# Two stacked cross-attention layers on one core: the key work of the second pair of batches moved by half a slot

## Chip, cores, metric

The kernel runs on one core of a Trainium2 chip. The metric is the device time of one execution in microseconds. It is taken as the median of several executions. All engines named below are those of the one core: PE (matrix products), ACT (scalar engine), DVE (vector engine), POOL (GpSimd), and SP, which here only issues DMA transfers. ACT issues a few small transfers too.

## What is computed

Two cross-attention layers follow each other. The input x has 16 batches of 256 positions and 320 channels; the context has 16 batches of 256 rows of 512, of which the first layer takes 77 rows as text and the remaining 179 as image tokens, and the second layer takes all but the last 4 rows as text. There are 20 heads of 16 channels. The first layer, cut to what matters:

```python
q = hidden_states @ Wq
k_text = text @ Wk
v_text = text @ Wv
probs = softmax(einsum('bhqd,bhkd->bhqk', q_h, k_h) * scale)
text_out = einsum('bhqk,bhkd->bhqd', probs, v_h)
ip_k = ip @ Wk_ip
ip_v = ip @ Wv_ip
scores = einsum('bhqd,bhkd->bhqk', q_h, ip_k_h) * scale
text_probs = softmax(einsum('bqc,bkc->bqk', q, k_text) * scale)
q_sem = einsum('bqk,bkc->bqc', text_probs, text)
sem = einsum('bqc,bnc->bqn', q_sem, ip) * scale
ip_probs = softmax(scores + SEM_SCALE * sem[:, None]) * spatial_mask
hs = text_out + einsum('bhqk,bhkd->bhqd', ip_probs, ip_v_h)
out = hs @ Wout + bout + residual
```

The second layer is built alike, with a semantic term per head that is normalised, and takes the first one's output.

## The kernel before

**Precision.** Every large product is made of three products of halves. A float32 operand is cast to a high half by ACT (line 147), and the rest is subtracted out as a low half by DVE or POOL (line 148). `prod` (line 205) then adds high by high, high by low and low by high: with four tiles of the contraction that is 12 matrix instructions into one PSUM bank.

**Slots.** A slot is one group of four heads of one batch; layer 0 has 80 slots (16 batches of 5 groups), layer 1 another 80. The main loop at the end of `xattn2` goes through the slots and issues for each of them a fixed sequence. In layer 0 (`slot0`) this is: the row maxima of slot k+1 turned on PE and sent into the query stack by four small DMAs issued by ACT (`maxima0`, L660, L662, L664); the scores of slot k+2, with two reductions by DVE (`score0`, L652, L653, L654); the turned scores of slot k (L676) with two exponentials on ACT (L679) and two multiplies on POOL (L682); then the fill point k+0.2; the weighted sum of slot k-1 (`attend0`, L709) with a transpose and small operations on DVE (`settle0`, L720 to L726) and a small add on POOL (L727); scores and turned scores for the second half of the rows; the loads of the stacks of slot k+4 on SP (`stacks0`); and the fill points k+0.6 and k+1.0.

**Tasks.** All other work is put into generators, called tasks. Each has a list of due times in slots, one for each of its steps (`task`, line 962). At a fill point (`fill`, line 990) every step that is due runs, earliest due time first. A step that needs another task's result runs that task as far as needed. Tasks that matter here are, for a pair of batches c: `k0` (keys and image keys of the pair, `keys0`), `q0` (queries of one batch, `queries0`), `m0t` and `v0` (token products and values), `s0` (semantic term), `c0` (closing of a batch).

**The steps of `k0` for the second pair (c = 1).** `context` loads four tiles of the context in its first step. Each of the next four steps splits one tile into halves, one cast on ACT and one subtraction on DVE (`halves`). Then come six steps, each with 12 products, a split of the result and either a copy on POOL (L318, after the text keys) or two stores of the keys to DRAM issued by SP (`keys_out`, after the image keys). The text keys' products have `wA` as their weights in the profile and 192 columns, the image keys' have `wB` and 360. The pair's keys are first read back by the stack loads issued in slot 6.

**Queries.** A batch's `q0` loads x into `xq`, splits it into `hq` (cast on ACT L517, low part on POOL L518, third tile on DVE L519), and projects it in three steps of 8 products (L528, `hq` by `wE`). The closing of a batch gathers the heads' output into `hT` (L739), splits it into `ho` (ACT L517, DVE L518, L519) and projects that (L528, `ho` by `wF`).

**Order.** The instructions of PE stand in the order in which the loop issues them. For the main loop the order of ACT, DVE, POOL and SP is set by a scheduler that estimates when each instruction will be ready; only within the start-up (`begin`) are these four pinned too. Each engine executes its own instructions in order. Two score banks (`T`), one bank for weighted sums (`P`), three for everything else (`X`) and one double bank for scores (`S`) are in PSUM; the loads of raw weights and context go through two buffers `rawc` and two buffers `raw`, each of which is free again when its subtraction is done; the keys go through two buffers `kst`.

The list of due times that the change touches, and the task that uses it:

```python
FIRST = {"k0": [-1, 0.2, 0.6, 0.6, 1, 1.2, 1.6, 1.6, 2, 2.2, 2.6], "s0": [...]}
task(("k0", c), FIRST["k0"] if c == 1 else shifted(n, ...), ...)
```

The pairs c = 2 to 7 take their times from `shifted`, and are not touched. Toward the end of layer 0, tasks `w6` and `w2` load the weights of the second layer (`wB` again for the image values, from `in_wvi`; `wE` for the queries, from `in_wq`) through the same `rawc` buffers.

Of the kernel before, what the change touches and what calls it, by code (L numbers as in the profile page):

```python
# [48 lines left out]
def xattn2(  # L49
# [249 lines left out]
    def keys0(c):  # L299
        if c not in ct0:  # L300
            tiles = context(2 * c, 2, 0.25)
            yield next(tiles)
            get("v0", 2 * c - 1)
            get("m0t", 2 * c - 1)
            ct0[c] = yield from tiles
        ct = ct0[c]
        kt = kts[c] = buf("kb", [128, 3, 2, 2, 96], FR, name="kt")
        for m in range(3):
            ms = slice(m * 128, (m + 1) * 128)
            kst = buf("kst", [128, 2, 2, S], FR, bufs=SIZES["KST"])  # L310
            for w, lo, hi, a, z in ((wk0, 0, 96, 0, T0), (wki0, T0 - 1, S, T0, S)):
                kp = bank()[:, : 2 * (hi - lo)].rearrange("p (b t) -> p b t", b=2)
                prod(kp, lambda s, k: w(s, k, ms), lambda s, k: ct(s, k)[:, :, lo:hi], 4)
                halves(kst[:, 0, :, a:z], kst[:, 1, :, a:z], kp[:, :, a - lo : z - lo])
                if a:
                    keys_out(kd[0][c], m, kst)
                else:
                    nc.gpsimd.tensor_copy(kt[:, m, :, :, :T0], f(kst[:, :, :, :T0]))  # L318
                yield
# [642 lines left out]
    def task(key, times, make, *needs):  # L962
        tasks[key] = [times, 0, make, needs, len(tasks)]
# [38 lines left out]
    def shifted(n, *times):  # L1002

        return [RAMP(n + t) for t in times]

    resid0 = []

    FIRST = {"k0": [-1, 0.2, 0.6, 0.6, 1, 1.2, 1.6, 1.6, 2, 2.2, 2.6], "s0": [-1, -1, -1, -1, -1, 0.2, 0.6]}
    for c in range(B // 2):
        n, k = 10 * c, [("k0", c)] if c else []  # L1010
        task(("k0", c), FIRST["k0"] if c == 1 else shifted(n, -14.4, -13.3, -13, -12.4, -12, -10.8, -10.4, -9.8, -9.4, -8.8, -8.4), (lambda c=c: keys0(c)) if c else keys_first,
             *([("w4", 0)] if c > 1 else []))
# [172 lines left out]
```

## Time and profile before

| | |
|---|---|
| median of 3 runs | 1636.12 us (1634.38, 1636.12, 1638.09) |
| the profiled execution's own time | 1630.48 us |
| its span, first to last instruction | 1628.7 us |
| PE busy | 1533.9 us (94%) |
| PE weight loads | 1232.8 us (76%) |
| DVE busy | 1209.1 us (74%) |
| POOL busy | 1189.4 us (73%) |
| ACT busy | 830.2 us (51%) |
| mean granted clock of PE | 0.974 |
| main chain that ended last | PE 52%, DVE 15%, POOL 11%, DMA 9%, ACT 6% |

Busy shares of PE overstate its work, since matrix instructions overlap. Over 40 equal slices PE is at nine tenths or more in most; the lower ones are the first (start-up), the 14th, 16th and 17th, and these lie between 529 and 692 us; layer 1's first slot begins at 744.0 us. The clock row of the page shows 9 nearly everywhere, 7 in the second slice (41 to 81 us) and 8 in the 17th and the last. Slot 0 begins at 55.1 us, slot 1 at 62.3, slot 2 at 84.7, slot 3 at 96.4 and slot 4 at 101.4.

How to read what follows: a timeline line gives the start in us, the length, the engine, the line of the kernel, the operation and its tiles, and how many of a kind follow each other; in brackets the idle time of the engine ahead of it and what ended it. "ACTq" and "SPq" are the issuing of transfers by these engines.

### The profile page before, as it was taken

The page shows a single profiled execution, that of the slowest core. Times are in us where ns is not written, and L with a number is a line of the kernel's source. Part 1 is how long each engine was busy: PE and PEld are TensorE (multiplying, and loading weights), DVE is VectorE, ACT ScalarE, POOL GpSimd, SP SyncE. Part 2 cuts the span into 40 slices and gives each one's busy share as a digit, 9 for nine tenths or more (in the row PEclk, how much of TensorE's full clock was granted, in tenths as well). Part 3 has the DMA queues.
Part 4 walks back from the last instruction along what each step waited for, and adds up shares of the span by engine and source line. Part 5 has one row for each costly group of instructions (what it writes and reads, how often), then busy time and mean ns, then how long its engine had stood idle before and what let it go on. Part 6 is the DMA issues. An engine that isn't in the chain of part 4 may idle for free.

```text
span 1628.7 us, 36230 instructions
## 1 busy us (share of the span) xinstructions
PE 1533.9 (94%) x13306; PEld 1232.8 (76%) x13306; DVE 1209.1 (74%) x2410; ACT 830.2 (51%) x1797; POOL 1189.4 (73%) x1147
## 2 busy tenths in 40 slices
PE   7899999999999898789999999999999999999996
PEld 6677878787878777577777777777777777777765
DVE  5567777777777668778877787778777877778685
ACT  5345455555555545445555555555554555555462
POOL 3358787878787767777678767866877687668676
PEclk9799999999999999899999999999999999999998
DMA  7767677767676666665514342433244334323301
GB/s 218 201 203 203 199 193 219 202 204 206 202 208 198 181 206 172 164 187 171 159 62 129 108 139 84 135 110 125 89 134 120 110 103 127 127 89 102 108 26 45
DMA packets 235741, 243.06 MB, mean 149 GB/s; under 512 B 19050, under 2 KB 219468, under 8 KB 235564
## 3 DMA queue, kind: packets, MB, share of 16 engines
q1 hardware_dynamic: 233356, 239.44, 49.4%
q8 instruction: 106, 1.74, 0.4%
q10 hardware_dynamic: 2208, 1.30, 0.3%
q14 instruction: 71, 0.58, 0.1%
HBM read 116.78 MB, written 88.18 MB: 126 GB/s over the span
## 4 chain that ended last, share of the span: by engine, by line
PE 52%; DVE 15%; POOL 11%; DMA 9%; ACT 6%; issue 4%; SPq 2%; ACTq 0%; POOLq 0%; DVEq 0%
PE X L205 15%; PE X L814 9%; PE X L528 7%; PE P L709 5%; POOL wt L805 4%; PE S L652 3%; POOL P L682 3%; PE P L823 3%; DMA qs<-qd 3%; PE P L826 2%; PE T L676 2%; PE T L775 2%; DVE wt L815 2%; DMA kd<-kst 2%; DVE mn L781 2%
## 5 line engine op out<-in xcount | busy, mean ns | idle before, releaser
L682 POOL TENSOR_TENSOR P<-P,rs 128x512 f32<-128x512 f32 x320 | 413.2, 1312 | 157.4 <-ACT P L679 157.0
L805 POOL TENSOR_TENSOR wt<-P,ctb 128x512 f32<-128x512 f32 x320 | 422.4, 1336 | 120.3 <-ACT ctb L804 118.7
L814 PE MATMUL X<-ctb,gm 128*128 128x512 f32 x1120 | 328.8, 411 | 2.5 <-DVE wt L815 2.5
L679 ACT ACTIVATE P<-T 128x512 f32<-128x512 f32 x320 | 175.9, 595 | 221.4 <-PE T L676 106.1
L786 ACT ACTIVATE P<-T 128x512 f32<-128x512 f32 x320 | 174.2, 597 | 144.1 <-PE T L775 123.3
L815 DVE TENSOR_TENSOR wt<-X,wt 128x512 f32<-128x512 f32 x320 | 216.7, 678 | 24.9 <-PE X L814 22.5
L804 ACT ACTIVATE ctb<-P 128x512 fp32r<-128x512 f32 x320 | 195.7, 631 | 73.1 <-PE X L814 57.9
L814 PEld LDWEIGHTS X<-ctb,gm 128*128 128x128 f32 x1120 | 188.8, 188 | 49.4 <-DVE wt L815 5.2
L781 DVE TENSOR_REDUCE mn<-S 128x4 fp32r<-128x1008 f32 x160 | 191.1, 1195 | 0.8 <-PE S L780 0.8
L654 DVE TENSOR_REDUCE mn<-S 128x4 fp32r<-128x716 f32 x160 | 142.6, 891 | 0.0
L676 PE MATMUL T<-qs,ks 127*128 127x256 f32 x640 | 112.1, 295 | 22.0 <-DMA qs<-mt 10.2
L709 PE MATMUL P<-P,vr 128*32 128x256 f32 x1920 | 129.4, 404 | 2.2 <-DVE mx L581 2.2
L652 PE MATMUL S<-ks,qs 125*128 125x256 f32 x640 | 117.4, 307 | 5.4 <-DVE mn L654 2.0
L652 PEld LDWEIGHTS S<-ks,qs 125*128 125x128 f32 x640 | 88.2, 194 | 41.8 <-issue 34.0
L894 POOL TENSOR_TENSOR r<-u,rs 128x40 f32<-128x40 f32 (+2 forms) x17 | 108.7, 6394 | 14.8 <-DVE u L891 14.7
L528 PE MATMUL X<-ho,wF 128*128 128x256 f32 x768 | 112.8, 290 | 6.4 <-DVE ho L518 3.0
L528 PE MATMUL X<-hq,wE 128*128 128x256 f32 x768 | 110.1, 287 | 7.5 <-ACT hq L517 3.2
L676 PEld LDWEIGHTS T<-qs,ks 127*128 127x128 f32 x640 | 92.8, 198 | 27.0 <-DVE tmp L726 11.6
L528 PEld LDWEIGHTS X<-ho,wF 128*128 128x128 f32 x768 | 103.5, 195 | 12.1 <-DVE ho L518 4.7
L528 PEld LDWEIGHTS X<-hq,wE 128*128 128x128 f32 x768 | 102.4, 193 | 12.0 <-ACT hq L517 3.6
L205 PE MATMUL X<-cta,wA 128*128 128x252 f32 (+1 forms) x720 | 100.6, 286 | 8.7 <-ACT wA L147 6.3
L205 PEld LDWEIGHTS X<-cta,wA 128*128 128x128 f32 x720 | 93.8, 194 | 15.2 <-ACT wA L147 6.5
(197 smaller groups left out, 2807.5 us busy)
## 6 DMA issues: line engine op xcount, KB each, us to landing
qd<-q SPq DMA_DIRECT2D x96, 384.0 KB
qs<-tph SPq DMA_DIRECT2D x64, 308.0 KB
kd<-kst SPq DMA_DIRECT2D x73, 256.0 KB
rawc<-in_cT_dram SPq DMA_DIRECT2D x60, 256.0 KB
qs<-qd SPq DMA_DIRECT2D x80, 192.0 KB
ks<-kd SPq DMA_DIRECT2D x80, 192.0 KB
ks<-kd SPq DMA_DIRECT2D x160, 96.0 KB
qs<-qd SPq DMA_DIRECT2D x160, 96.0 KB
```

Source lines behind the costliest of these rows:

```text
L205: last = mm(out, lhs(a, k), rhs(b, k), start=i == 0, stop=i == len(terms) - 1)
L528: mm(pp, w(s, k, slice(m * 128, (m + 1) * 128)), a[:, t], start=i == 0, stop=i == len(terms) - 1)
L652: mm(sp[:, h], Q[: XROW + T0, h, t * 128 : (t + 1) * 128], K[: XROW + T0, h], start=True, stop=True)
L676: mm(st[p][:, j], K[:KS0, 2 * p + j, t * 128 : (t + 1) * 128], Q[:KS0, 2 * p + j], start=True, stop=True)
L679: exp = anchor(nc.scalar.activation(pt, st[p], AF.Exp, scale=SCALE))
L682: anchor(nc.gpsimd.tensor_mul(pt, pt, rs[:, t : t + 1].to_broadcast([128, 2, S])))
L709: mm(pv[32 * s : 32 * s + 32, o : o + S], v[:, vt, h : h + 32], P[k, s // 2][:, t, s % 2], start=vt < 2, stop=vt != 1,)
L781: anchor(nc.vector.tensor_reduce(maxes[k + 2][:, t], sp[:, :, :T1], axis=AX.X, op=ALU.max))
L804: nc.scalar.activation(R[k, u][:, t], P[k, u][:, t], AF.Copy, scale=0.5)
L805: anchor(nc.gpsimd.tensor_sub(W[k, u][:, t], P[k, u][:, t], f(R[k, u][:, t])))
L814: mm(yp, gm[:, gb], R[k, u][:, kt], start=i == 0, stop=i == len(blocks[n]) - 1)
L815: nc.vector.tensor_mul(W[k, u][:, n], yp, W[k, u][:, n])
```

## The change

One list of eleven due times is replaced. Nothing else is edited; the number of instructions on PE is the same.

```diff
-    FIRST = {"k0": [-1, 0.2, 0.6, 0.6, 1, 1.2, 1.6, 1.6, 2, 2.2, 2.6], "s0": [-1, -1, -1, -1, -1, 0.2, 0.6]}
+    FIRST = {"k0": [-1, 0.6, 0.6, 1, 1.2, 1.6, 2, 2, 2.2, 2.6, 2.6], "s0": [-1, -1, -1, -1, -1, 0.2, 0.6]}
```

Step by step, for the second pair's keys (m is the third of the key channels):

| step | due before | due now |
|---|---|---|
| loads of four context tiles | -1 | -1 |
| halves of tiles 1, 2, 3, 4 | 0.2, 0.6, 0.6, 1 | 0.6, 0.6, 1, 1.2 |
| text keys, image keys, m = 0 | 1.2, 1.6 | 1.6, 2 |
| text keys, image keys, m = 1 | 1.6, 2 | 2, 2.2 |
| text keys, image keys, m = 2 | 2.2, 2.6 | 2.6, 2.6 |

On PE this puts the first 12 key products behind slot 1's weighted sum and its second scores and turned scores, and the later ones behind what stood after them, the first step of the queries of batch 2 among it. On the other four engines the scheduler decides anew; its order differs from the one before in slots 1 to 3, in some single places of later slots, and in a stretch around the change of layers (from about slot 68 to slot 85).

## The prediction

> **What bounds the kernel now.** I read the page's busy shares first (PE 94% of the span), then the clock over the first 240 us, then TensorE's own timeline where the moved work stands, then the queues that feed it. The edit touches the second to fourth slot, 63 to 101 us of the span. There PE is not limited by its work: it waits in short gaps, and for 20 us it runs at half clock. First the windows of 4 us; the third number from the end is the granted clock:
>
> ```profile
> 64.00:68.00 4.00, 3.47 (x12) 2.70 (x12) 1.97 (x4) 2.62 (x6) 0.55 (x1) 0.50 0.96 320
> 72.00:76.00 4.00, 4.00 (x29) 2.10 (x30) 0.86 (x2) 0.29 (x1) 0.44 (x1) 0.50 0.22 61
> 76.00:80.00 4.00, 4.00 (x26) 4.00 (x26) 2.71 (x7) 2.27 (x4) 2.31 (x2) 0.81 0.17 49
> ```
>
> The clock is 0.50 until about 77.2, though PE has no gap after 71.94: some 5.3 us of unbroken work before it comes back. The timeline of PE (start, length, instruction, and in brackets the idle time before it):
>
> ```profile
> 66.78 0.96 PE L205 MATMUL X<-cta,wA 128*128 128x192 f32 x3 [0.20 <-DVE cta L148]
> 68.57 0.74 PE L205 MATMUL X<-cta,wA 128*128 128x192 f32 x2 [0.84 <-DVE cta L148]
> 70.25 1.03 PE L205 MATMUL X<-ctb,wA 128*128 128x192 f32 x3 [0.73 <-DVE ctb L148]
> 71.94 0.74 PE L205 MATMUL X<-ctb,wA 128*128 128x192 f32 x2 [0.66 <-DVE ctb L148]
> 72.61 2.79 PE L709 MATMUL P<-P,vr 128*32 128x256 f32 x24
> ...
> 81.77 0.51 PE L528 MATMUL X<-hq,wE 128*128 128x256 f32 x2 [0.82 <-POOL hq L518]
> ```
>
> The first twelve key products wait four times for context halves (2.43 us together) and hold up L709, whose inputs POOL had finished at 64.54. The query projection L528 waits 0.82 for POOL. What stands before it on ACT and POOL:
>
> ```profile
> 70.09 3.63 ACTq L664 DMA_DIRECT2D qs<-mt  x3
> 73.82 0.29 ACT L147 CAST kst<-X 128x154 fp32r<-128x154 f32 x1 [3.12 <-DMA qs<-mt]
> 77.01 1.09 ACT L679 ACTIVATE P<-T 128x512 f32<-128x512 f32 x2 [2.90 <-PE T L676]
> 77.98 0.84 ACT L517 CAST hq<-xq 128x768 fp32r<-128x768 f32 x1
> ```
>
> ACT issues three small DMAs until 73.72, and only then serves the slot's exponentials, the hq cast and, through POOL, hq's low half.
>
> **First place: slots 0 to 3.** By the order of both programs, PE's instructions are the same in number; the key products move behind L709, S and T of slot 1, and eight of the query products now come before 24 of the key products.
> - Removed: the four gaps, 0.20 + 0.84 + 0.73 + 0.66 = 2.43 us. L709 starts at 66.0, ends at 68.7 (2.7 at half clock), S takes 1.15, T 0.85: 70.7.
> - The moved products then wait only for the last low half. DVE now does it behind the transpose (0.72) and two reduces (1.3) of that slot: from 70.2 to 72.1, then 0.7 to 1.15. The products end at 73.2.
> - Added: the query products come next. ACT is free at 73.72; two exponentials 1.09, hq cast 0.84: 75.6. POOL: two multiplies 2.80 from 74.4, the small add 0.45 that now stands between them, hq 1.27: 78.7. One product can go at 75.7, the rest at 78.7. The gap is 73.2 to 78.7, 5.5 less 0.2, where before it was 2.43 + 0.82 = 3.25: 2.1 us more. Behind the waiting instruction stand 24 key products and slot 2's L660, S and T; ACT's and POOL's next slot waits for these.
> - The clock: by the rows above it is back some 4.5 to 5.3 us after work resumes, near 83.5. Until then seven query products take 1.5 and twelve key products 3.4 (before, at 78.34, six took 1.14). Adding up: m1's twelve 1.32, L660/S/T 1.15, twelve 1.97, L709 1.43, S and T 1.15 give 90.6 for the T that ended at 89.87. That is +0.7, and twelve products (1.32) are still to do: +2.05 at the start of slot 3 (96.41 before).
> - What follows can swallow part. In slots 3 and 4 PE waits 1.50 for DVE and 2.20 before L709 at 106.77. Both hang on ACT's cast of wF at 100.02, which stands behind slot 3's exponentials; these follow PE by 2 us, and lose 0.7 of that in the DMA issue that was late anyway (98.91). I take **+1.4**. Low end -0.5: were the three DMA issues 0.57 each, as at 85.61, instead of 1.21, everything from ACT on would be 1.9 earlier. High end +2.6: nothing swallowed and the clock back 0.5 later.
> - DMAs moved: two key stores per third, 0.5 to 4 us later on SP, behind the load of xq now (0.86 to issue). Their reader, slot 6's stack, comes some 20 us after; cover is ample, and without it the price would be one such store's landing, 5 us. The kst casts and subtractions (0.29 to 0.53 each) fall on ACT and DVE while PE is the later one: nothing.
>
> The Trainium skill, "TensorE: Matmul & The Clock Gate" (section "Why this matters for your kernels"), asks for no PE-idle gaps above about 3 us, since one idle window sends the clock to half: that speaks against putting four short gaps into one. By its window of about 3.4 us the half-rate work would cost 1.7 us; this trace, where gaps of 0.7 to 1.9 us were enough to keep 0.50 for 20 us, makes it 2.2 to 2.6.
>
> **Second place: the change of layers.** The scheduler places all engines but PE, and its different start shifts two decisions near 650 to 690 us:
>
> ```profile
> 667.09 0.62 ACT L147 CAST wB<-rawc 128x512 fp32r<-128x512 f32 x1 [2.75 <-DMA rawc<-in_wvi_dram]
> ...
> 674.27 0.83 ACT L517 CAST ho<-hT 128x768 fp32r<-128x768 f32 x1 [1.08 <-DVE hT L739]
> ...
> 678.27 0.51 PE L528 MATMUL X<-ho,wF 128*128 128x256 f32 x2 [0.20 <-DVE ho L519]
> ...
> 684.41 0.23 PE L660 MATMUL X<-ident_r,mn 128*8 128x128 f32 x1 [2.04 <-DVE mn L654]
> ```
>
> - The third load of value weights now stands ahead of four stack loads on SP (issued 661.05 before, some 656.2 now, since DVE's subtraction that frees its buffer goes ahead of the transpose). Its 6 us then end at 661 to 662, ACT does not sit 2.75 us, and the T that ended at 667.04 ends near 663.5: -3.5.
> - Against it, the layer output ho is made later: POOL's copy L729 stands behind two more multiplies (2.5), the transpose L739 behind a subtraction of wE (1.56), ACT's cast behind another cast and two DMA issues. Working through: cast at 677.4, last part by DVE at 680.4, with PE ready at 674.5. PE idles 3.7 and then starts at half clock: the eight products end at 680.7 instead of 678.7, L709 2.72 and S 1.15 instead of 1.43 and 0.66, reduces 1.3: the L660 of 684.41 comes at 686.1. I take **+1.7**. Ends: -3.3 if ho is in time and the head start stays; +3.5 if ho is late and the early load gains nothing.
>
> **Third place: first stacks of layer 1.** On SP one of the three query stores now goes behind the load of xc (issue 1.18). The query rows, loaded at 759.06, wait for all three; ACT waited 4.18 for these, PE 0.51. I take **+1.0**, ends 0 and +2. The other swaps (single transposes, small adds) stand beside PE work of 1.4 to 3.5 us: nothing, or one instruction's 0.4 us each without that cover.
>
> **The sum.** 1.4 + 1.7 + 1.0 = +4.1 us. On the profiled execution's own 1630.48 (span 1628.7 and 1.8 around it) that is 1634.6; that execution is 5.6 below the median of the three runs, 1636.12, so the forecast is 1640.2. Later slots pass a delay on: they are a chain of PE and its feeders without slack that depends on the start.
>
> **The rivals.**
> - A, the forecast: 1640.2, own range 1637 to 1644. For it: PE stops at hq and at ho, each with its supplier's place in the queue. Chance 0.55, of which 0.10 falls within 0.2%.
> - B, not slower: the early weight load wins. Place: 656 to 676 us. Price: the head start of 3.5 us stays, with 1.4 paid at the start: 1634.0. It decides if ho's cast still comes by about 674.5. For it: the 2.75 us wait of ACT and 20 us without PE between 640 and 720 (by windows of 20 us), so there is something to win. Against it: the chain that makes ho is already 0.20 late today. Chance 0.22: 0.13 faster, 0.09 within.
> - C, the change does nothing that lasts: the waits of 1.50 and 2.20 swallow the start and the second place is level: 1636.1 to 1637.5. Against it: those waits hang on ACT, which follows PE. Chance 0.13.
> - D, all high ends: 2.6 + 3.5 + 2.0 = 8.1: 1644.2. For it: half clock was held for 20 us once. Chance 0.10.
>
> **How the numbers follow.** 0.2% is 3.3 us, about what a measurement of this kernel can tell. Slower: 0.45 + 0.10 = 0.55. Within: 0.10 + 0.09 + 0.13 = 0.32. Faster: 0.13. The sums of the ends are -0.5 - 3.3 + 0 = -3.8 (1632.3) and +8.1 (1644.2); with the spread of a median the range is 1632 to 1645.
>
> **What would show it.** Right: L709 of slot 0 near 66; one PE gap of 4 to 6 us before an L528 with the releaser POOL hq L518; clock 0.50 again in 79 to 83; slot 3's L660 some 2 us late; the third weight load issued before 658; a PE gap of 3 us or more before L528 on ho. Wrong: ACT's three DMA issues taking 1.7 us, or hq's low half before 76; ho's cast before 675; the layer-1 start earlier than before by more than 1 us.

## The result, and the profile after

| | changed | before |
|---|---|---|
| median | 1637.05 us (1632.61 to 1646.04, 12 runs) | 1633.47 us (1628.77 to 1638.09, 12 runs) |
| ratio | 1.0025, 95% interval 1.0013 to 1.0037 | |
| the profiled execution | 1646.04 us, span 1644.2 | 1630.48 us, span 1628.7 |

The change costs 3.6 us between the medians. A second measurement beside the experiments gave 1.0036 (1.0022 to 1.0049). The profiled execution of the changed kernel is the longest of its twelve, so its 15.5 us more than the profiled one of before are mostly not the change, and the traces must be compared stage by stage. For that I use the starts of L660 (L792 from row 80 on, in layer 1); each row has two such products, and the start of a row is here that of the second. A row is named by the slot whose maxima L660 makes; the instruction stands in the slot before, so the prediction's "slot 3's L660" is row 4. In the expectations below, slot numbers from 60 on are rows. Start of a row, less the same in the first trace of before (us):

| row | 0 | 2 | 4 | 6 | 42 | 66 | 72 | 74 | 76 | 78 | 84 | 157 |
|---|---|---|---|---|---|---|---|---|---|---|---|---|
| changed, first trace | 4.10 | 4.11 | 5.48 | 3.31 | 8.13 | 9.05 | 3.95 | 9.69 | 11.17 | 15.67 | 14.81 | 14.83 |
| changed, second trace | 2.50 | 2.50 | 3.36 | 1.14 | 2.22 | 3.12 | -1.59 | 5.37 | 6.90 | 9.40 | 8.55 | 8.62 |

Rows 0 to 2 lie before the change, and rows 6 to 66 have the same order of PE: what comes up there differs from one execution to the next. Both traces agree on two things: nothing is left of the start by row 6 (0.8 and 1.4 us less than at row 2), and 5.4 to 5.8 us come up between rows 66 and 84, at the change of layers.

PE at the start (timeline of the changed kernel: start, length, instruction, idle time ahead and what ended it):

```profile
68.52 2.18 PE L709 MATMUL P<-P,vr 128*32 128x256 f32 x24
...
75.16 0.47 PE L205 MATMUL X<-ctb,wA 128*128 128x192 f32 x2 [1.81 <-DVE ctb L148]
78.14 0.58 PE L528 MATMUL X<-hq,wE 128*128 128x256 f32 x1 [2.51 <-ACT hq L517]
81.40 1.86 PE L528 MATMUL X<-hq,wE 128*128 128x256 f32 x7 [2.69 <-POOL hq L518]
83.06 2.00 PE L205 MATMUL X<-cta,wB 128*128 128x360 f32 x6
```

L709 no longer waits behind the key products. These now wait 0.17 and 1.81, and the query product behind them waits for the ACT and then the POOL part of hq, 2.51 and 2.69. The windows of the same trace (third number from the end: granted clock) show what follows:

```profile
72.00:76.00 4.00, 1.65 (x11) 1.13 (x9) 3.87 (x8) 0.15 (x1) 1.84 (x2) 1.00 0.61 119
76.00:80.00 4.00, 0.58 (x1) 0.29 (x1) 0.71 (x2) 2.00 (x4) 3.05 (x3) 0.60 0.61 169
80.00:84.00 4.00, 2.60 (x11) 2.60 (x12) 0.29 (x1) 0.37 (x1) 1.74 (x3) 0.50 0.55 145
```

The clock reads 1.00 while PE has 1.65 us of work in 4, 0.60 while it has 0.58, and 0.50 when the work comes. ACT's timeline shows why hq is late, as forecast:

```profile
71.54 4.69 ACTq L664 DMA_DIRECT2D qs<-mt  x3
76.28 1.09 ACT L679 ACTIVATE P<-T 128x512 f32<-128x512 f32 x2 [4.12 <-DMA qs<-mt]
77.25 0.83 ACT L517 CAST hq<-xq 128x768 fp32r<-128x768 f32 x1
```

The change of layers, in the timeline of the changed kernel, engines together:

```profile
661.73 0.79 PE L676 MATMUL T<-qs,ks 127*128 127x256 f32 x2 [3.87 <-DVE tmp L726]
...
669.06 0.62 ACT L147 CAST wB<-rawc 128x512 fp32r<-128x512 f32 x1 [0.55 <-DMA rawc<-in_wvi_dram]
...
682.78 3.41 DVE L148 TENSOR_TENSOR wE<-rawc,wE 128x384 fp32r<-128x384 f32 x1
686.12 0.43 DVE L739 STREAM_TRANSPOSE hT<-hsn 128x256 f32<-128x256 f32 x1
686.58 0.83 ACT L517 CAST ho<-hT 128x768 fp32r<-128x768 f32 x1 [3.22 <-DVE hT L739]
687.47 2.59 PE L528 MATMUL X<-ho,wF 128*128 128x256 f32 x8 [5.45 <-ACT ho L517]
...
731.60 0.77 PE L676 MATMUL T<-qs,ks 127*128 127x256 f32 x2 [3.84 <-DVE P L724]
```

ACT's wait for the value weights falls from 2.75 to 0.55: the early load works, and row 72 is 5.1 us better than row 66 (4.7 in the second trace). Then PE waits 5.45 for ho, and the gain is gone by row 74. Both were forecast. The last line was not: 3.84 us before the last two of the four products of T (two banks of two), and 2.25 in the second trace, where the trace of before has the four in one piece. It has a wait of the same kind earlier, as the changed kernel has (the second trace of the changed kernel, then two lines of the trace of before):

```profile
725.57 0.48 PE L676 MATMUL T<-qs,ks 127*128 127x256 f32 x2 [2.25 <-DVE P L724]
```

```profile
652.04 0.80 PE L676 MATMUL T<-qs,ks 127*128 127x256 f32 x2 [3.98 <-DVE tmp L726]
...
717.59 0.63 PE L676 MATMUL T<-qs,ks 127*128 127x256 f32 x4
```

T reads qs and ks, which are there. What it waits for on DVE is a reader of P or S, which is no operand of T: the sign of a shared buffer. The built programs tell which PSUM bank each tile was given. The banks are not fixed per kind of tile (the numbers of banks given above for T, P, X and S say only how many of each may be in use at once); the scheduler hands out the eight of them by its own estimate of when each is free:

| tile | what its bank held last, before | what its bank held last, changed | PE's idle time ahead of it |
|---|---|---|---|
| T, row 70, first half, second bank | the last P | the last P | 3.98; changed 3.87 and 3.86 |
| X of L528 on ho, row 73 | a T | the last P | 0; changed 5.45 and 5.50, under the wait for ho |
| T, row 76, second half, first bank | the S just made | the S just made | 1.47; changed 1.47 and 1.47 |
| T, row 77, second half, second bank | a T | the S just made | 0; changed 3.84 and 2.25 |

S is read by L653 and L654. At row 77 these stand behind the split of the layer output (timeline of DVE, changed kernel):

```profile
727.22 1.54 DVE L518 TENSOR_TENSOR ho<-hT,ho 128x512 fp32r<-128x512 f32 x1
728.68 1.48 DVE L519 SCALAR_TENSOR_TENSOR ho<-ho,tmask,hT 128x256 fp32r<-128x256 f32 x1
730.08 0.25 DVE L723 RECIPROCAL P<-nt 128x16 f32<-128x16 f32 x1
730.24 0.41 DVE L653 TENSOR_REDUCE mn<-S 128x4 fp32r<-128x308 f32 x1
730.58 0.88 DVE L654 TENSOR_REDUCE mn<-S 128x4 fp32r<-128x716 f32 x1
```

L654 ends at 731.46, and T starts at 731.60; the releaser printed, L724, is merely the next on DVE. So there are two candidates for the cost at the change of layers: the order of the instructions, as forecast, or the banks.

### The profile page after: what moved, and what is told of

It reads as the page before. It is cut to its first block, busy times and chain, and to the rows that moved or that the text cites. A ratio compares the mean times of both kernels' runs of the same rounds, so it can differ in the third digit from the quotient of the medians.

```text
span 1644.2 us, 36224 instructions
## 1 busy us (share of the span) xinstructions
PE 1540.4 (94%) x13306; PEld 1240.0 (75%) x13306; DVE 1208.7 (74%) x2410; ACT 830.8 (51%) x1797; POOL 1188.2 (72%) x1147
## 4 chain that ended last, share of the span: by engine, by line
PE 54%; DVE 15%; POOL 10%; DMA 8%; ACT 5%; issue 4%; SPq 1%; ACTq 0%; POOLq 0%; DVEq 0%
PE X L205 17%; PE X L814 9%; PE X L528 7%; PE P L709 5%; POOL wt L805 4%; PE S L652 3%; PE P L823 3%; PE T L676 3%; POOL P L682 3%; PE P L826 3%; PE T L775 2%; DMA qs<-mt 2%; DVE wt L815 2%; DVE mn L781 2%; DVE ho L518 2%
## 5 line engine op out<-in xcount | busy, mean ns | idle before, releaser
L654 DVE TENSOR_REDUCE mn<-S 128x4 fp32r<-128x716 f32 x160 | 142.6, 891 | 0.0
L709 PE MATMUL P<-P,vr 128*32 128x256 f32 x1920 | 130.2, 407 | 1.5 <-DVE mx L581 1.5
L528 PE MATMUL X<-hq,wE 128*128 128x256 f32 x768 | 114.2, 294 | 13.1 <-ACT hq L517 6.1
L528 PE MATMUL X<-ho,wF 128*128 128x256 f32 x768 | 113.3, 291 | 11.7 <-ACT ho L517 6.9
L528 PEld LDWEIGHTS X<-hq,wE 128*128 128x128 f32 x768 | 106.0, 200 | 17.5 <-ACT hq L517 6.6
L528 PEld LDWEIGHTS X<-ho,wF 128*128 128x128 f32 x768 | 103.7, 195 | 17.7 <-ACT ho L517 7.8
L205 PEld LDWEIGHTS X<-cta,wA 128*128 128x128 f32 x720 | 95.2, 197 | 13.2 <-ACT wA L147 5.9
```

Source lines behind the costliest of these rows:

```text
L205: last = mm(out, lhs(a, k), rhs(b, k), start=i == 0, stop=i == len(terms) - 1)
L528: mm(pp, w(s, k, slice(m * 128, (m + 1) * 128)), a[:, t], start=i == 0, stop=i == len(terms) - 1)
L709: mm(pv[32 * s : 32 * s + 32, o : o + S], v[:, vt, h : h + 32], P[k, s // 2][:, t, s % 2], start=vt < 2, stop=vt != 1,)
```

## The experiments

Four kinds of edit. "Held" means that order dependencies fix the order of ACT, DVE, POOL and SP to a recorded one (they add no wait of their own; the added lines shift the line numbers by 13, so L689 is T, L541 the query product, L673 is L660). A held order also makes the scheduler hand out other banks.

### Start and rest apart, at held order

```diff
+ORDER = [[...], [...], [...], [...]]
...
         fill(999)
+    for chain in ORDER:
+        for one, two in zip(chain, chain[1:]):
+            queued(SimpleInst(nc.get_inst_by_name(two)), SimpleInst(nc.get_inst_by_name(one)))
```

The changed list with the order of before from slot 4 on:

> The changed kernel, with every instruction of ACT, DVE, POOL and SP from slot 4 on held to the order that they have in the kernel before; so only the start (slots 0 to 3) differs from before. Forecast (first place +1.4, the rest +2.7): +1.4 us on the kernel before, ratio 1.0009; slot 3's L660 some 2 us late against slot 0, and 1.4 late from slot 6 on. Rival 'swallowed': the start costs nothing by slot 6 (within 0.5 us), and the time is that of before. Rival 'all of it is the start': +3 to +4 us, ratio 1.002.

Measured: 1629.77 us, ratio 0.9985 (0.9974 to 0.9996). The old list with the order of the changed kernel from slot 4 on:

> The kernel before, with every instruction of ACT, DVE, POOL and SP from slot 4 on held to the order that they have in the changed kernel; so the start is that of before and the change of layers that of the changed kernel. Forecast: +2.7 us (ratio 1.0017), 1.7 of it by slot 80 and 1.0 after. Rival 'the change of layers makes all of it': +3.6 us (ratio 1.0022). Rival 'the early weight load wins': -2 us or more. Between the starts of slots 66 and 72 a gain of some 5 us on before, lost again at slot 74 where L528 waits for ho.

Measured: 1629.25 us, 0.998 (0.9966 to 0.9994). Each half alone is a gain, which no theory had allowed for: holding the order had itself changed something. The two controls, each kernel held to its own order:

> The kernel before, with every instruction of ACT, DVE, POOL and SP from slot 4 on held to the order that it has there anyway. The order is that of before on every engine; what comes out differently is which PSUM bank each tile of T, P and X gets from slot 6 on. Theory 'bank' (a T placed in the bank of the P before it waits until DVE has read that P): the wait of 3.98 us before T in slot 71 goes, slots 66 to 84 are 2 us or more shorter than in the trace of before, and the time is 2.5 to 4 us lower (ratio 0.998). Theory 'order' (only the place of the instructions counts): the time of before within 0.7 us.

Measured: 1625.73 us, 0.9964 (0.9949 to 0.998).

> The changed kernel, held in the same way to its own order, with other PSUM banks from slot 6 on. Theory 'bank': the waits for L726 and L724 before T (3.9 us in slot 71, 2.3 to 3.8 in slot 78) are absent, and the time is 1.5 to 4 us below the kernel before (ratio 0.998). Theory 'order': 3.6 us above before (1.0022) as the changed kernel is. With the three other held kernels it gives the start and the rest apart at equal banks: start = this less the second kernel of the first series, forecast +1.4; rest = this less the first kernel of the first series, forecast +2.7.

Measured: 1631.75 us, 0.9995 (0.9975 to 1.0015). The kernel before gains 6 us with no instruction moved on any engine, only banks. Its trace (PE's timeline) has no wait at the place of the 3.98:

```profile
642.94 0.64 PE L689 MATMUL T<-qs,ks 127*128 127x256 f32 x4
644.18 2.79 PE L722 MATMUL P<-P,vr 128*32 128x256 f32 x24 [0.60 <-POOL P L695]
```

The four products of T of row 70 follow each other, and the weighted sum L722 (L709 elsewhere) comes 0.60 later. Theory "order" is refuted. The other three kernels held in this way differ from it in banks only at the start and at the change of layers. At these banks the start costs 0.0021 (first kernel less third) or 0.0015 (fourth less second), the rest 0.0016 or 0.0010: about 3 and 2 us, each uncertain by some 2.5.

### The due time of one cast

```diff
-    FIRST = {"k0": [-1, 0.2, 0.6, 0.6, 1, 1.2, 1.6, 1.6, 2, 2.2, 2.6], "s0": [...]}
+    FIRST = {"k0": [-1, 0.6, 0.6, 0.6, 1, 1.2, 1.6, 1.6, 2, 2.2, 2.6], "s0": [...]}
```

> Only the due times of the two cast steps are moved (0.2 to 0.6), those of the key products stay. The start then has the order of before on all engines, and only the change of layers comes out in a third order. If the start is what costs: the time of before, within 1.5 us. If the order at the change of layers is what sets the time, it may differ from before by up to 3 us either way, all of it between slots 66 and 84.

The edit moves only the first of the four cast steps; "the two cast steps" in the expectation says too much. Measured: 1636.63 us, 1.0025 (1.0015 to 1.0036), as dear as the whole change, with the start's order unaltered on every engine. Its trace loses 6.5 us between rows 66 and 84, 4.2 of it at one place (timeline, PE and DVE):

```profile
677.26 1.50 DVE L519 SCALAR_TENSOR_TENSOR ho<-ho,tmask,hT 128x256 fp32r<-128x256 f32 x1
678.68 0.16 DVE L724 TENSOR_TENSOR P<-P,mk 128x8 f32<-128x8 f32 x1
678.76 1.53 DVE L148 TENSOR_TENSOR wE<-rawc,wE 128x384 fp32r<-128x384 f32 x1
...
681.42 0.40 DVE L726 TENSOR_TENSOR tmp<-nt,P 128x256 f32<-128x256 f32 x1
681.97 2.05 PE L528 MATMUL X<-ho,wF 128*128 128x256 f32 x8 [4.05 <-DVE tmp L726]
```

ho is complete at 678.76, and DVE's order up to here is that of before, where L528 started without waiting and stopped once, for 0.20. Here its X was given the bank of the last P, and waits 3.2 us longer, until L726 has read P. This is the cleanest view of the mechanism: another bank at the same order.

### Other banks at the change of layers alone

The hold of above over the change of layers only: order as built everywhere, banks as built up to row 69.

> The changed kernel with ACT, DVE, POOL and SP held to its own order only around the change of layers. Order and PSUM banks are those of the changed kernel everywhere but for the banks of the tiles in slots 68 to 84. Theory 'bank': 5 to 7 us below the changed kernel (ratio to before 0.998 to 0.9995), all of it between slots 68 and 80: the wait of T for L726 (3.9 us at 661) and that for L724 (2.3 to 3.8 us at 726 to 732) are gone. Theory 'order': 3.6 to 5.9 us above before (1.0025 to 1.0036), as the changed kernel.

Measured: 1632.1 us, 0.9986 (0.9972 to 1.0001). That is 0.0039 and 0.0050 under the two measurements of the changed kernel, 6 to 8 us. Its timeline of PE has none of the three waits of T (row 70, 76 and 77):

```profile
648.99 0.92 PE L689 MATMUL T<-qs,ks 127*128 127x256 f32 x4
...
708.04 0.64 PE L689 MATMUL T<-qs,ks 127*128 127x256 f32 x4
...
722.04 0.65 PE L689 MATMUL T<-qs,ks 127*128 127x256 f32 x4
```

Rows 66 to 84 take 159.40 us here, 163.28 and 162.95 in the changed kernel: 3.7 of the 6 to 8 us are seen; the rest is within what executions differ by.

> The kernel before, with the same hold around the change of layers on its own order; only the banks in slots 68 to 84 are others. Theory 'bank': 2 us below before by the stage (ratio 0.9985), since only the wait of 3.98 before T at 652 is there to be removed. If it is 5 us or more, as in the run held from slot 4 on, the banks of the slots before count for nothing; if it is 2, those 3 us more came from slots 6 to 66. Its distance to the run of the changed kernel with other banks is what start and order cost at equal banks: forecast +4.1, by the stages of the ten traces +1.7.

Measured: 1629.8 us, 0.9988 (0.9974 to 1.0002): 2 us, as expected from the one wait removed, though the interval just reaches 1. So some 4 of the 6 us of the kernel held from slot 4 on probably came from rows 6 to 66. The traces point the same way: 498.3 us there on average (494.8 to 501.2) in six traces of kernels held from slot 4 on, 501.0 (498.3 to 505.0) in six with the banks as built there. One place shows it in every trace, row 60 (PE; the trace of before, then that of the same kernel held from slot 4 on):

```profile
557.75 1.23 PE L676 MATMUL T<-qs,ks 127*128 127x256 f32 x4 [5.89 <-DVE tmp L726]
```

```profile
555.92 2.79 PE L722 MATMUL P<-P,vr 128*32 128x256 f32 x24 [2.03 <-DVE tmp L739]
```

As built, the first bank of this T held the last P, and T waits 5.88 to 6.13 us for L726 in all six traces. Held from slot 4 on, T has the bank of an earlier T and does not wait for it; the next P got the bank of the last P, and the weighted sum waits 2.03 to 2.24 us for that same reader (L739 there). From row 60 to row 61 it is 16.7 us (16.1 to 17.2) against 14.1 (13.2 to 15.1), in ranges that do not overlap.

### One bank kept for P

```diff
+    own = {"P": ps.tile([128, 512], F32, tag="P", name="P", bufs=1)}
     def bank(tag="X"):
-        return ps.tile([128, 512], F32, tag=tag, name=tag, bufs=BANKS[tag])
+        return own[tag] if tag in own else ps.tile([128, 512], F32, tag=tag, name=tag, bufs=BANKS[tag])
```

> The kernel before with one PSUM bank kept for P alone, so that T and X share five banks and never follow P. The order at the change of layers comes out in a further version. Theory 'bank': no wait of T or L528 for L726 or L724 anywhere; 2 to 4 us below before (0.998). Rival: five banks for T and X make new waits of PE for ACT or DVE in each slot, 0.02 us or more a slot: 3 us or more above before.

Measured: 1629.9 us, 0.9991 (0.9973 to 1.0008).

> The changed kernel with one PSUM bank kept for P alone. Theory 'bank': within 1.5 us of the run of before with its own bank, so that the change itself is worth little once the banks are fixed. Forecast (start +1.4 and order +2.7): 4.1 us above that run.

Measured: 1630.06 us, 0.9988 (0.9973 to 1.0003). Inconclusive in part: both are near 2 us below before and level with each other, as theory "bank" has it, but both intervals reach 1, and order and banks differ between the two, at the change of layers and elsewhere. The bank of its own also moves the wait instead of ending it: T and X no longer wait for a reader of P, but the next weighted sum does (L711 and L728 are L709 and L726 elsewhere; trace of the kernel before with this edit), 4.01 us here and 3.54 with the changed list:

```profile
660.18 2.36 PE L711 MATMUL P<-P,vr 128*32 128x256 f32 x20 [4.01 <-DVE tmp L728]
```

### The gap before hq

In the changed list, 24 key products are moved ahead of the query product that waits; from slot 4 on the order of before is held.

```diff
-    FIRST = {"k0": [-1, 0.6, 0.6, 1, 1.2, 1.6, 2, 2, 2.2, 2.6, 2.6], "s0": [...]}
+    FIRST = {"k0": [-1, 0.6, 0.6, 1, 1.2, 1.6, 1.87, 1.87, 2.2, 2.6, 2.6], "s0": [...]}
```

> Slots 0 to 3 as in the changed kernel, but 24 more key products stand before the query product that waits for hq, where the changed kernel has PE idle for 3.8 to 7 us; from slot 4 on the order and the banks of the run of before that was held. Theory 'gap before hq': the wait before L528 falls under 2 us and slot 3 starts 2 to 4 us earlier than in the changed kernel's start (1.7 us on the trace of before, mean of five, against -0.4 to -2.3 here); time 1625 to 1628, level with the held run of before or 1.5 below. Rival 'half clock': the products run at half speed in the gap, ACT and POOL wait for their banks, hq comes later by as much, and slot 3 starts no earlier than in the changed kernel.

Measured: 1622.69 us, 0.9934 (0.9918 to 0.995): faster than both kernels. Its PE timeline:

```profile
73.45 0.47 PE L218 MATMUL X<-ctb,wA 128*128 128x192 f32 x2 [1.81 <-DVE ctb L161]
73.76 1.78 PE L218 MATMUL X<-cta,wB 128*128 128x360 f32 x6
75.33 2.00 PE L218 MATMUL X<-ctb,wB 128*128 128x360 f32 x6
77.13 0.97 PE L218 MATMUL X<-cta,wA 128*128 128x192 f32 x6
77.95 0.83 PE L218 MATMUL X<-ctb,wA 128*128 128x192 f32 x6
78.62 1.46 PE L541 MATMUL X<-hq,wE 128*128 128x256 f32 x8
```

The query products follow without a gap. Part of the fill does run at half clock (2.00 for six products against 1.15 later), but the time was free. Rows 2 to 4 take 29.95 us in this one trace, 36.1 on average in the changed start. The rival falls. For comparison, the kernel before at the same hold, once more:

> The kernel before held to its own order from slot 4 on, once more, to set beside the fill: 6 us below before (ratio 0.9964) if the first measurement of it holds; 2 to 3 us (0.998) if it was on the lucky side of its interval.

Measured: 1625.61 us, 0.9961 (0.9947 to 0.9974). The filled start is 0.0027 below that, 4 us under the start of before. Against the changed start at the same hold (0.9985, in the first series) the fill is worth 0.0051, some 8 us. And the changed kernel once more:

> The changed kernel once more, beside the two halves of it: +3.6 us on before (ratio 1.0022). If the two parts add up, the excess of the first two kernels sums to the excess of this one within 1.5 us. Its trace against the first one of the same kernel shows how much of a slot-by-slot difference is not the change: at least 4 us at slot 0, by the first pair of traces.

Measured: 1639.13 us, 1.0036 (1.0022 to 1.0049). The parts did not sum as expected, because the halves ran at other banks.

## Why the prediction was right, and where it was not

The forecast was +4.1 us; +3.6 and, in the second measurement, 1.0036 times as long were measured. Its sum is right, but not all of its terms, and that the sum came so close is partly luck: a term of 3 to 5 us that it did not have (the banks) and sizes that cancel stand beside a third place with the wrong sign. The 1640.2 it gave as a time is 3.1 above the measured 1637.05, since it started from the 1636.12 of three runs where twelve gave 1633.47. For the same reason rival C's 1636.1 to 1637.5 holds the measured median, but C meant that nothing lasts, and the interval of 1.0013 to 1.0037 is clear of 1. The traces of the kernels with one of the two starts give the stages (us, mean and range):

| stage | before | changed | difference | forecast |
|---|---|---|---|---|
| rows 2 to 4 (seven and six traces) | 32.8 (30.6 to 34.6) | 36.1 (35.0 to 37.8) | +3.3 | +2.05 |
| rows 2 to 6 | 50.8 (48.4 to 53.3) | 52.4 (50.7 to 54.5) | +1.6 | +1.4 |
| rows 66 to 84, banks as built (one and two) | 157.5 | 163.1 | +5.6 | +1.7, and +1.0 for SP |
| rows 66 to 84, other banks (five and three) | 155.8 (154.3 to 159.0) | 157.0 (155.7 to 159.4) | +1.2 | |

With the banks as built the stages add up to +7.2, where 3.6 and, by the second ratio, 5.9 were measured: they rest on few traces, and the ranges of rows 2 to 6 overlap.

- **First place, right in mechanism.** L709 early, the gap before L528 with releaser POOL hq L518, the half clock in 80 to 84 and the late row 4 are all there. Two sizes were off and cancel. The moved products were to end at 73.2 without a gap; their last low half made a gap of 1.7 us on average instead (1.24 to 1.82 in six traces), because DVE does it behind the transpose and the reduces. And the waits of the next slots swallowed 1.7 us, not 0.65: those of 1.50 and 2.20 in the trace of before are 0.71 and 1.47 in the changed one. The fill shows that the gap before hq was the price.
- **Second place, right as far as it was seen.** Set back by the 9.05 of row 66, the weight load is issued at 656.6 (forecast 656.2) and ho is cast at 677.5 (forecast 677.4). Row 74 against row 66 is +0.6 and +2.25 (forecast +1.7). At other banks the gap stays near the forecast 3.7: the two waits before and within L528 on ho add up to 3.3 to 3.9 in three traces. The subtraction of wE ahead of the transpose took 3.41 us and not 1.56, which PE's own head start (5.1 us, not 3.5) paid for. Rival B, the early load, was there for two rows and was lost as forecast, since ho was late.
- **What the prediction lacked.** The step that failed is "the scheduler places all engines but PE, and its different start shifts two decisions": it also places the tiles in banks. From row 74 to row 84 come another 5.1 and 3.2 us, largely the wait of T for S's readers and the half clock after it. It was a term of its own, and the largest of the change as built: at other banks the order of this stage costs +1.2 us, with ranges that overlap.
- **Third place, wrong in sign.** From row 82 to row 84, where the query rows are waited for, the changed kernel is 0.76 and 0.74 us shorter, not 1.0 longer. It had been judged from a place in SP's queue alone. The sign goes with the order in every trace: 22.6 to 22.9 us in five with the changed kernel's order there, 23.4 to 25.8 in six with that of before. What made it shorter was not traced further.
- **Still open.** What start and order cost at like banks: +5 us by the kernels held from slot 4 on, level by those with other banks at the change of layers alone and by those with P's own bank, each uncertain by 3 to 4 us. By stages it is 1.6 and 1.2.

## What to carry to other kernels

When an engine waits for a reader of a tile that is none of its operands, it is probably waiting for a buffer: look up what stood in that buffer before it. Where a scheduler places tiles, a small edit early in the kernel can move the buffers of a place 600 us later, so judge it by stages and by controls that hold the order, of the old kernel too, before its cost or gain is put down to what it was meant to do. A wait for a late operand was worth filling here with work that was already there, even at half clock.

## What the hardware showed besides

- PE's granted clock fell to half after gaps shorter than 3 us. In the kernel with the fill, gaps of 0.83, 0.25 and 1.81 us within 6 us, the rest of it filled, were followed by half clock for over 3 us (about 74.1 to 77.5). The Trainium skill, "TensorE: Matmul & The Clock Gate" (section "Why this matters for your kernels"), asks only for no gap above about 3 us; here no single gap was that long. Windows of 1 us, granted clock third from the end:

```profile
73.00:74.00 1.00, 0.55 (x4) 0.55 (x5) 0.93 (x4) 0.19 (x1) 0.00 (x0) 1.00 0.20 58
74.00:75.00 1.00, 1.00 (x5) 1.00 (x4) 0.23 (x1) 1.00 (x3) 0.52 (x1) 0.53 0.71 203
76.00:77.00 1.00, 1.00 (x5) 1.00 (x4) 0.36 (x2) 0.00 (x0) 1.00 (x2) 0.50 0.85 240
77.00:78.00 1.00, 1.00 (x9) 1.00 (x8) 0.14 (x1) 0.46 (x1) 1.00 (x2) 0.76 0.88 206
```

- The same start, with the same order on every engine, took from 48.4 to 53.3 us between rows 2 and 6 in seven executions. Three small DMA issues of ACT took 3.63 us together in the trace of before and 4.69 in that of the changed kernel, where a single one takes 0.57 elsewhere.
- Some subtractions on DVE took far longer beside POOL's multiplies, but not each. L518 on ho took 0.69 and 1.54 us, L519 0.48 and 1.48, at two places of the changed kernel's trace; POOL is idle at the first and multiplies at the second. Yet in the trace of before L518 on ho took 0.70 at 676.08, beside a multiply. The Trainium skill, "GPSIMD Engine Reference" (section "Specifications"), says that DVE instructions with two operands in SBUF contend with POOL; the 3.41 us of the subtraction of wE beside POOL's work, 0.51 for the same shape at 686.48 with POOL idle, fit that, and no run here separates the two engines.
